# Attention block in float32: five pairs of output tiles projected by seven block products instead of eight, values of the tokens broadcast one by one

## The chip, the cores and the metric

The kernel runs on one core of one Trainium2 chip. The metric is the device time of one execution in microseconds, the median over several runs. The engines are TensorE (PE; its weight loads are listed as PEld), VectorE (DVE), ScalarE (ACT), GpSimd (POOL) and SyncE (SP, which here only issues DMAs).

## What is computed

Sixteen samples of 100 rows and 640 columns attend to a context of 722 rows and 384 columns, of which the last four are "tokens" with a path of their own. Everything is float32.

```python
query = hidden_states @ Wq
keyt = enc @ Wk                      # enc: the first 718 rows of the context
valt = enc @ Wv
hs = _mha(query, keyt, valt)         # 8 heads of 80
ca_q1 = jnp.einsum('btc,th->bch', ca, Wq_ca)     # ca: the last 4 rows
indices = np.linspace(0, CROSS_ATTENTION_DIM - 1, unet_size).astype(np.int64)
ca_q1 = ca_q1[:, indices, :]
ca_hs1 = _mha(ca_q1, residual, residual)
ca_q2 = ca_hs1 @ Wq
ca_k2 = ca @ Wk_ca
ca_v2 = ca @ Wv_ca
ca_hs2 = _mha(ca_q2, ca_k2, ca_v2)
out = (hs + ca_hs2) @ Wout + b_out + residual
```

The change concerns the last line, and how `ca_v2` reaches the engine that uses it.

## The kernel before

After a prologue that loads and prepares the weights, a loop runs over the 16 samples (`for b in range(B)`, L1122). Inside the loop the order of the instructions on every engine is the order in which they are written (a manual schedule, L1121); each engine works through its own list, and semaphores make it wait where data or a buffer is missing.

One sample on TensorE: scores (L620, three groups), the small products of the token path (L808, L746), the transposes of the sample before (L923), then the value and key blocks (L440, L471, interleaved; the next sample's keys are made here), the last chunk of keys (`last_keys`, L565), the output projection of a finished row tile if there is one (L951), the queries of the next two samples (L541, odd b only) and the attention products (L1317).

Output tiles. The 1600 output rows are cut into eleven tiles of 128 rows, one of 64 and one of 128 (`OC`, L33). A tile ends in sample `ENDS[r]`; `O_AFTER` (L37) says after which sample it is projected, so that no sample takes two of the full tiles. The samples of attention results are transposed (`transpose`, L916) into `hsT` tiles of five chunks of 128 columns by 128 rows. `load` of class `Last` (L897) brings the rows of x into `xn` and has GpSimd add the bias. `project` (L941) multiplies the five chunks with the two halves of Wout, ten matmuls of 128x128 by 128x320 into two banks of a PSUM pair; VectorE adds both halves to `xn` in one instruction (L970), and SyncE writes the rows out.

The order of things near the projection of a sample with 0 < b < 15 (L1237 to L1267) is `softmax3`, `values2`, value and key blocks, `subtract` and `exponential` of the three score tiles, `second.load`, `loads`, `load_m`, the third `subtract` and `exponential`, `last_keys`, `load_rest`, `second.softmax1`, `last.project`. Behind it GpSimd makes the masked keys (`keys`) and the sums of the context that the block products need (`enc_sums`).

Token path on GpSimd. `scores1` (L774) writes the first scores into `e1`; `Maximum` finds the row maximum and spreads it, where the last copy runs on VectorE, or on ScalarE if `scalar` is set. `load` of class `Second` (L824) broadcasts the values of the four tokens, 4x640 numbers, to 100 partitions: one DMA of 1000 KB from GpSimd's queue into `vb`, one sample ahead. `values2` (L861) does four products and three adds of 100x640 on GpSimd. `products` and `copy` (L740, L764) fill `y`, for which there are two buffers, as for `ca`.

PSUM has three pools of two buffers each: pairs of banks (`pair`), and single banks `psumk` and `psum1`; `psum` takes them in turn. The value and key blocks already use bilinear schemes with fewer products than blocks (`V_PLAN`, `K_PLAN`, L101 to L119).

Of the kernel before, what the change touches and what calls it, by code (L numbers as in the profile page):

```python
# [8 lines left out]
F32 = mybir.dt.float32  # L9
AF = mybir.ActivationFunctionType  # L10
ALU = mybir.AluOpType
# [4 lines left out]
NH, D = 8, 80  # L16
CAD, T = 384, 4
SK = 722 - T
P = 128
# [16 lines left out]
ENDS = [(lo + n - 1) // S for lo, n in OC]  # L36
O_AFTER = [b + 1 if b % 2 == 0 and b + 1 not in ENDS else b for b in ENDS]  # L37
HT = NH * T
# [94 lines left out]
def kernel(  # L133
# [66 lines left out]
    def hsT_tile(name):  # L200
        return main.tile([P, HC, P], F32, tag="hsT", name=name, bufs=2)

# [3 lines left out]
    def vb_tile(name):  # L206
        return main.tile([P, T, H], F32, tag="vb", name=name)

# [54 lines left out]
    wout_sb = const.tile([P, HC, H], F32, name="wout_sb")  # L263
    bias = const.tile([P, H], F32, name="bias")

    wvca_sb = enc_tile("wvca").rearrange("p f k -> p (f k)")[:, : CC * H].rearrange(
# [23 lines left out]
    load_first(0, CC, 2, slice(0, KT))  # L290
    tokens = vb_tile("tokens")
    cat_sb = tokens[:, CC, : CC * B * T].rearrange("p (c n) -> p c n", c=CC)
    wkca_sb = tokens[:, :CC, :]
    in_order(nc.sync.dma_start(out=cat_sb, in_=cat.rearrange("p c b t -> p c (b t)")))
# [6 lines left out]
    in_order(nc.sync.dma_start(out=xT, in_=xt[0:2].rearrange("b p c s -> p b c s")))  # L301
    ca_0 = small.tile([S, T, S], F32, tag="ca", name="ca_0", bufs=2)
    in_order(nc.sync.dma_start(out=ca_0, in_=cas[0].unsqueeze(0).to_broadcast([S, T, S])))
# [62 lines left out]

    ys = []
    for j in range(2):
        y = const.tile([S, NH, HT + 1], F32, name=f"y_{j}")
        nc.gpsimd.memset(y[:, :, HT:], 1.0)  # L370
        ys.append(y)

# [272 lines left out]
    def wait_for(ins, other):  # L645

        tc.add_manual_dep(
            ins.ins,
            other.ins.name,
            mybir.DependencyInfo(  # L650
                mybir.DependencyClass.Sync, mybir.DependencyReason.DATA
            ),
            reason="apart",
        )
# [70 lines left out]
    class Second:  # L725


        def __init__(self, b, xT, ca=None):
            self.b, self.xT = b, xT[:, b % 2]
            self.top = None  # L730

            self.ca = ca
            if ca is not None:
                return
            self.ca = small.tile([S, T, S], F32, tag="ca", name=f"ca_{b}", bufs=2)
            nc.sync.dma_start(
                out=self.ca, in_=cas[b].unsqueeze(0).to_broadcast([S, T, S])
            )
# [25 lines left out]
        def copy(self):  # L764
            b, y_ps = self.b, self.y_ps
            self.y = ys[b % 2]
            nc.scalar.copy(
                self.y[:, :, :HT].rearrange("p (u h) k -> p u h k", u=2),
                y_ps[:S, HT : 11 * HT].rearrange("p (u h k) -> p u h k", u=2, h=5)[
                    :, :, :4, :  # L770
                ],
            )
# [19 lines left out]
        def softmax1(self, n=8):  # L792

            if not self.top:
                self.top = Maximum(e1, f"1_{self.b}")
            self.top.go(n)
            if self.top.over is not None:
                nc.vector.tensor_tensor(e1[:S], e1[:S], self.top.over[:S], ALU.subtract)
# [24 lines left out]

        def load(self):  # L824
            b = self.b
            self.vb = vb = vb_tile(f"vb_{b}")
            nc.gpsimd.dma_start(
                out=vb[:S],
                in_=va_d[b * T : (b + 1) * T, :].unsqueeze(0).to_broadcast([S, T, H]),
            )  # L830

        def scores2(self):
# [28 lines left out]
        def values2(self, behind=None):  # L861

            b, p2, vb = self.b, self.p2, self.vb
            self.hs2 = hs2_tile(f"hs2_{b}")[:S]
            sums = self.hs2.rearrange("p (h d) -> p h d", h=NH)
            for t in range(T):
                to = sums if t == 0 else product_tile(f"hs2_{b}_{t}")[:S, :H].rearrange(
                    "p (h d) -> p h d", h=NH
                )
                first = nc.gpsimd.tensor_tensor(  # L870
                    to,
                    vb[:S, t, :].rearrange("p (h d) -> p h d", h=NH),
                    p2[:, :, t].unsqueeze(2).to_broadcast([S, NH, D]),
                    ALU.mult,
                )
                if t:
                    nc.gpsimd.tensor_tensor(sums, sums, to, ALU.add)  # L877
                elif behind:
                    wait_for(first, behind)

    def product_tile(name):
# [7 lines left out]
    class Last:  # L889
# [51 lines left out]
        def project(self, chunks=range(HC)):  # L941
            for r, xn in self.xn.items():
# [29 lines left out]
                )  # L972
                nc.sync.dma_start(out=o_v, in_=xn[:n])

        def project_few(self, r):
# [146 lines left out]
    for b in range(B):  # L1122
# [89 lines left out]
        elif b + 1 < B:  # L1212
# [4 lines left out]
            def both(n):  # L1217
                vv.go(n)
                kk.go(n)

            second.scores1(seen)
            if b == 1:
# [41 lines left out]
            if b + 2 < B:  # L1264
                enc_next = load_rest(b + 2, enc_next)
            second.softmax1()
            last.project()  # L1267
        else:
# [127 lines left out]
```

## Time and profile before

| what | value |
|---|---|
| runs | 943.98, 946.33, 944.89 us; median 944.89 |
| span of the profiled execution | 942.4 us |
| ScalarE busy | 364.7 us (39%) |
| mean granted clock of TensorE | 1.000 |
| TensorE in the first 60 us / 60 to 920 / the last 22.4 | 57.6 / 858.2 / 18.7 us busy |
| mean DMA rate, share of the span | 66 GB/s |
| attention products, L1317, from 204.82 (b = 2) | 6.67 us |
| GpSimd idle before `scores1`, L781, in all | 145.2 us, of which 125.0 until VectorE's maximum (L1156) |
| SyncE waiting to issue the next enc load, L228 | 598.8 us in 13 waits, for the value products |

The profile is of one execution, whose span runs from the first to the last instruction; the runs are timed from outside. A line of a timeline or of a group gives engine, line of the kernel, operation, what it writes and reads, the shapes and a count ("x20"); "idle before" is the time in which the engine had nothing to run, with the instruction that ended it. A float32 matmul leaves two records, each with its weight load.

### The profile page before, as it was taken

The page shows a single profiled execution, that of the slowest core. Times are in us where ns is not written, and L with a number is a line of the kernel's source. Part 1 is how long each engine was busy: PE and PEld are TensorE (multiplying, and loading weights), DVE is VectorE, ACT ScalarE, POOL GpSimd, SP SyncE. Part 2 cuts the span into 40 slices and gives each one's busy share as a digit, 9 for nine tenths or more (in the row PEclk, how much of TensorE's full clock was granted, in tenths as well). Part 3 has the DMA queues.
Part 4 walks back from the last instruction along what each step waited for, and adds up shares of the span by engine and source line. Part 5 has one row for each costly group of instructions (what it writes and reads, how often), then busy time and mean ns, then how long its engine had stood idle before and what let it go on. Part 6 is the DMA issues. An engine that isn't in the chain of part 4 may idle for free.

```text
span 942.4 us, 25629 instructions
## 1 busy us (share of the span) xinstructions
PE 934.5 (99%) x11215; PEld 796.2 (84%) x11215; DVE 674.0 (72%) x1084; ACT 364.7 (39%) x605; POOL 623.1 (66%) x565
## 2 busy tenths in 40 slices
PE   9999999999999999999999999999999999999998
PEld 6998979888797888989789887987989888897866
DVE  3559794977929688595955959578693886949684
ACT  1244443524334244433424334244431534334241
POOL 5857976776738757495873948657694576748514
PEclk9999999999999999999999999999999999999999
DMA  8822024040310404003050130403113030210300
GB/s 264 296 60 87 3 70 128 1 130 3 94 60 1 117 2 135 5 11 122 1 151 3 37 82 1 139 1 95 38 40 113 1 112 7 59 53 1 95 8 29
DMA packets 45367, 62.48 MB, mean 66 GB/s; under 512 B 13448, under 2 KB 37320, under 8 KB 43656
## 3 DMA queue, kind: packets, MB, share of 16 engines
q1 hardware_dynamic: 41720, 42.97, 15.2%
q0 software_dynamic: 2512, 16.72, 6.1%
q8 instruction: 88, 1.44, 0.6%
q10 hardware_dynamic: 1024, 1.15, 0.4%
q14 instruction: 23, 0.19, 0.1%
HBM read 55.26 MB, written 5.57 MB: 65 GB/s over the span
## 4 chain that ended last, share of the span: by engine, by line
PE 96%; DVE 3%; issue 0%; DMA 0%; ACT 0%; POOL 0%; ACTq 0%; DVEq 0%
PE s_ps L620 12%; PE a_ps L1317 12%; PE v_psA L440 10%; PE v_psB L440 8%; PE kT_ps L565 8%; PE k_psA L471 7%; PE q_ps L541 7%; PE o_ps L951 7%; PE k_psB L471 6%; PE v_psC L440 3%; PE k_psC L471 3%; PE y_ps L746 2%; PE v_ps L381 2%; PE v_psD L440 2%; PE v_psE L440 2%; PE k_psE L471 1%
## 5 line engine op out<-in xcount | busy, mean ns | idle before, releaser
L781 POOL TENSOR_TENSOR e<-ca,g 100x800 f32<-100x800 f32 x64 | 99.8, 1570 | 145.2 <-DVE most L1156 125.0
L870 POOL TENSOR_TENSOR hs<-vb,p 100x640 f32<-100x640 f32 x64 | 105.6, 1659 | 45.9 <-DVE p L856 32.5
L877 POOL TENSOR_TENSOR hs<-hs,hs 100x640 f32<-100x640 f32 x48 | 113.9, 2373 | 3.8
L1317 PEld LDWEIGHTS a_ps<-vs,st 120*36 120x36 f32 (+3 forms) x3072 | 109.1, 125 | 5.6 <-issue 5.5
L1317 PE MATMUL a_ps<-vs,st 120*36 120x81 f32 (+3 forms) x3072 | 111.9, 233 | 0.0
L440 PE MATMUL v_psA<-wv_sb,enc 128*120 128x320 f32 x352 | 109.5, 434 | 0.0
L506 POOL TENSOR_TENSOR enc<-enc 128x240 f32<-128x240 f32 x135 | 98.1, 736 | 16.9 <-DMA enc<-in_enct 9.8
L1144 DVE TENSOR_TENSOR st<-st,over 120x1600 f32<-120x1600 f32 x48 | 107.6, 2243 | 0.0
L637 ACT COPY st<-s_ps 120x800 f32<-120x800 f32 x64 | 49.7, 829 | 135.6 <-PE s_ps L620 135.6
L620 PE MATMUL s_ps<-qp,kT 32*120 32x100 f32 x3072 | 97.4, 263 | 0.0
L620 PEld LDWEIGHTS s_ps<-qp,kT 32*120 32x120 f32 x3072 | 94.7, 179 | 1.6 <-issue 0.2
L788 POOL TENSOR_TENSOR e<-e,e 100x800 f32<-100x800 f32 x48 | 90.4, 1884 | 3.8
L440 PE MATMUL v_psB<-wv_sb,enc 128*120 128x320 f32 x296 | 91.9, 433 | 0.0
L471 PE MATMUL k_psA<-enc,wk_sb 128*128 128x240 f32 x360 | 87.6, 366 | 0.0
L1329 DVE RECIPROCAL rs<-a_ps 100x4 f32<-100x4 f32 x32 | 5.8, 182 | 111.0 <-PE a_ps L1317 111.0
L1156 DVE TENSOR_TENSOR most<-most,st 120x800 f32<-120x800 f32 x64 | 66.2, 1034 | 24.1 <-ACT st L631 23.0
L1152 ACT ACTIVATE st<-st 120x1600 f32<-120x1600 f32 x48 | 73.9, 1539 | 22.3 <-DVE st L1144 22.2
L471 PEld LDWEIGHTS k_psA<-enc,wk_sb 128*128 128x128 f32 x360 | 68.2, 190 | 16.8 <-DVE kT L411 0.2
L440 PEld LDWEIGHTS v_psA<-wv_sb,enc 128*120 128x120 f32 x352 | 63.2, 183 | 22.6 <-issue 0.5
L471 PE MATMUL k_psB<-enc,wk_sb 128*128 128x240 f32 x300 | 73.1, 366 | 0.3 <-DVE sm L853 0.3
L440 PEld LDWEIGHTS v_psB<-wv_sb,enc 128*120 128x120 f32 x296 | 54.0, 183 | 21.9 <-DVE vs L411 0.4
L541 PE MATMUL q_ps<-xT,wq_sb 128*128 128x200 f32 x400 | 69.1, 333 | 0.0
(146 smaller groups left out, 1732.8 us busy)
## 6 DMA issues: line engine op xcount, KB each, us to landing
vb<-va_d POOLq DMA_DIRECT2D x16, 1000.0 KB, 7.4
enc<-in_enct SPq DMA_DIRECT2D x30, 240.0 KB, 3.9
enc<-in_enct SPq DMA_DIRECT2D x15, 360.0 KB, 3.6
xT<-in_xt SPq DMA_DIRECT2D x8, 500.0 KB, 4.3
rest<-in_enct SPq DMA_DIRECT2D x31, 120.0 KB, 6.6
xn<-in_x SPq DMA_DIRECT2D x11, 320.0 KB, 5.7
out<-xn SPq DMA_DIRECT2D x11, 320.0 KB, 3.2
ca<-in_cas SPq DMA_DIRECT2D x16, 156.2 KB
```

The source lines that it names most:

```text
L440: nc.tensor.matmul(at[0][j][:KN, : H // 2], a_form(self.enc, f)[:, j * KN : (j + 1) * KN], wv_there.get(f, wv_sb[:, W_AT[f]]), start=first ...
L471: nc.tensor.matmul(at[:, i * KT : (i + 1) * KT], wk_sb[:, W_AT[f], i], a_form(self.enc, f), start=(first and i == 0), stop=last, skip_grou ...
L506: nc.gpsimd.tensor_tensor(out, left, right, op)
L541: nc.tensor.matmul(q_ps[:, : 2 * S].rearrange("p (j s) -> p j s", j=2), wq_sb[:, c, n * P : (n + 1) * P], xT[:, :, c, :], start=(c == 0), ...
L565: nc.tensor.matmul(bank[:, i * KT : (i + 1) * KT], weights[c], a_raw(enc, u, c), start=(i == 0 and c == 0), stop=(c == CC - 1), skip_group ...
L620: nc.tensor.matmul(s_ps[r][:n, 256 * a + lo : 256 * a + hi], kT[rows, c, u, j * KN : (j + 1) * KN], rhs, start=(a == 0 and c == 0), stop=( ...
L781: first = nc.gpsimd.tensor_tensor(to, self.ca[:, t, :].unsqueeze(1).to_broadcast([S, NH, S]), g[:, :, t].unsqueeze(2).to_broadcast([S, NH, ...
L788: nc.gpsimd.tensor_tensor(e, e, to, ALU.add)
L870: first = nc.gpsimd.tensor_tensor(to, vb[:S, t, :].rearrange("p (h d) -> p h d", h=NH), p2[:, :, t].unsqueeze(2).to_broadcast([S, NH, D]), ...
L877: nc.gpsimd.tensor_tensor(sums, sums, to, ALU.add)
L1144: return nc.vector.tensor_tensor(st[i], st[i], top.over[:KN].unsqueeze(1).to_broadcast([KN, 2, ROWS]), ALU.subtract,)
L1317: nc.tensor.matmul(a_v[lo:hi, h % 4], st[i // 2][: KEYS[i], i % 2, h * S + lo : h * S + hi], block(i, h // 4)[: KEYS[i], h % 4], start=(i ...
```

## The change

Ten of the eleven full tiles are taken in five pairs (`PAIRS`): a pair is projected in the sample after the second tile's end, that is in samples 3, 6, 8, 11 and 13. The first four chunks of the two tiles are seen as a matrix of 2x2 blocks (tile by two chunks), Wout's first four chunks as 2x2 blocks (two chunks by half of the columns). The 2x2 product is made by seven block products with sums of blocks; the fifth chunk goes the usual way. The sums of the tiles' blocks and one sum of the weights are made on GpSimd in the sample of the pair, partly in place; weight sums are formed once in sample 2, and one is undone in the sample after each pair. After the last pair the overwritten quarter of Wout is loaded again. For SBUF space `y` and `ca` get one buffer, and `vb` two buffers of one token each: the first two tokens are loaded by GpSimd's queue, the others by SyncE's when a product has freed a buffer. `wkca` moves into a part of `wk_sb`. `hsT` gets three buffers. The remaining tiles (64 rows, the last full ones) are projected as before.

```diff
+PAIRS = {ENDS[r + 1]: r for r in range(0, 10, 2)}
+O_AFTER = [ENDS[r | 1] if r < 2 * len(PAIRS) else ENDS[r] for r in range(len(OC))]
...
-        return main.tile([P, HC, P], F32, tag="hsT", name=name, bufs=2)
+        return main.tile([P, HC, P], F32, tag="hsT", name=name, bufs=3)
...
-        return main.tile([P, T, H], F32, tag="vb", name=name)
+        return main.tile([P, H], F32, tag="vb", name=name, bufs=2)
...
+    wout2 = const.tile([P, 2, 2, H // 2], F32, name="wout2")
+    sum1 = const.tile([P, 2, P], F32, name="sum1")
...
-            self.ca = small.tile([S, T, S], F32, tag="ca", name=f"ca_{b}", bufs=2)
+            self.ca = small.tile([S, T, S], F32, tag="ca", name=f"ca_{b}")
...
-                self.top = Maximum(e1, f"1_{self.b}")
+                self.top = Maximum(e1, f"1_{self.b}", self.b - 2 in PAIRS)
...
         def load(self):
+            self.vb = [self.piece(nc.gpsimd, t) for t in range(2)]
+
+        def piece(self, engine, t):
             b = self.b
-            self.vb = vb = vb_tile(f"vb_{b}")
-            nc.gpsimd.dma_start(
-                out=vb[:S],
-                in_=va_d[b * T : (b + 1) * T, :].unsqueeze(0).to_broadcast([S, T, H]),
-            )
+            vb = vb_tile(f"vb_{b}_{t}")
+            engine.dma_start(
+                out=vb[:S], in_=va_d[b * T + t].unsqueeze(0).to_broadcast([S, H])
+            )
+            return vb
...
                 elif behind:
                     wait_for(first, behind)
+                if t + 2 < T:
+                    self.vb.append(self.piece(nc.sync, t + 2))
...
+        def sums(self):
+            r = PAIRS[self.b]
+            one, two = hsTs[r], hsTs[r + 1]
+            for out, left, right, op in (
+                (sum1, two[:, :2], two[:, 2:4], ALU.add),
+                (two[:, :2], sum1, one[:, :2], ALU.subtract),
+            ):
+                nc.gpsimd.tensor_tensor(out, left, right, op)
+
+        def project_pair(self):
...
+            both = pair(f"o_ps_{r}")
+            b1, b2 = psumk(f"o_ps1_{r}"), psumk(f"o_ps2_{r}")
+            b3, b4 = both[:, 0], both[:, 1]
...
+            def read(bank, j, k):
+                part = xn[r + j][:, k * (H // 2) : (k + 1) * (H // 2)]
+                nc.vector.tensor_tensor(part, bank[:, : H // 2], part, ALU.add)
+
+            product(b1, [(one[:, :2], w(0, 0))], True)
+            read(b1, 0, 0)
+            product(b2, [(one[:, 2:4], w(1, 0)), (one[:, 4:], last(0))], True)
+            read(b2, 0, 0)
+            nc.gpsimd.tensor_tensor(one[:, 2:4], one[:, 2:4], two[:, :2], less)
+            product(b1, [(two[:, :2], wout2[:, 0])], False)
+            read(b1, 1, 0)
+            nc.gpsimd.tensor_tensor(two[:, :2], two[:, 2:4], two[:, :2], less)
+            nc.gpsimd.tensor_tensor(wout2[:, 0], wout2[:, 0], w(0, 0), less)
+            product(b4, [(two[:, 2:4], wout2[:, 1]), (two[:, 4:], last(0))], True)
+            read(b4, 1, 0)
+            product(b1, [(sum1, w(0, 1))], False)
+            read(b1, 1, 1)
+            product(b3, [(two[:, :2], wout2[:, 0])], True)
+            read(b3, 1, 0)
+            product(b1, [(one[:, 2:4], w(1, 1)), (one[:, 4:], last(1))], False)
+            read(b1, 0, 1)
+            product(b3, [(two[:, 4:], last(1))], False)
+            read(b3, 1, 1)
...
+            if b == 2:
+                for o, left, right in (
+                    (forms[1], forms[1], forms[0]),
+                    (wout2[:, 0], forms[3], forms[1]),
+                    (wout2[:, 1], forms[2], wout2[:, 0]),
+                ):
+                    nc.gpsimd.tensor_tensor(o, left, right, ALU.subtract)
+            elif last.b - 1 in PAIRS:
+                nc.gpsimd.tensor_tensor(wout2[:, 0], wout2[:, 0], forms[0], ALU.add)
             second.scores1(seen)
...
+            if last.b in PAIRS:
+                last.sums()
+                second.softmax1(3)
+                last.project_pair()
+                if last.b == max(PAIRS):
+                    nc.sync.dma_start(
+                        out=forms[1],
+                        in_=wout[: 2 * P, H // 2 :].rearrange("(c p) n -> p c n", p=P),
+                    )
             second.softmax1()
-            last.project()
```

`w(i, k)` is the block of Wout with chunks 2i and 2i + 1 and half k of the columns, `last(k)` its fifth chunk, `one` and `two` are the `hsT` tiles of the pair, `product` issues one matmul for each chunk of its terms, and `forms` lists w(0, 0), w(0, 1), w(1, 0), w(1, 1).

## The prediction

> **What bounds the kernel now.** I read the totals first, then the chain of work that ended last, then the timeline around one output projection, then the DMA issues.
>
> ```profile
> PE 934.5 (99%) x11215; PEld 796.2 (84%) x11215; DVE 674.0 (72%) x1084; ACT 364.7 (39%) x605; POOL 623.1 (66%) x565
> ...
> PE 96%; DVE 3%; issue 0%; DMA 0%; ACT 0%; POOL 0%; ACTq 0%; DVEq 0%
> ```
>
> TensorE is busy for 934.5 of 942.4 us, and 96% of the chain is TensorE: a matmul taken out of the loop counts in full unless another engine then makes TensorE wait. One stretch of that chain, in sample 3 of the loop (b = 3, which will hold the first pair), in order of time (start, us, what):
>
> ```profile
> 249.45 3.65 PE kT_ps L565 x18
> 253.10 5.38 PE o_ps L951 x20
> 258.48 8.46 PE q_ps L541 x50
> ```
>
> Twenty records are ten matmuls (each float32 matmul leaves two). So a 128x128 by 128x320 matmul costs 0.538 us here; in the timeline below the projection starts at 252.93 and the queries follow at 258.32, 5.39 us later, which agrees. The mean granted clock is 1.000. The same stretch on the other engines:
>
> ```profile
> 235.24 1.54 POOL L908 TENSOR_TENSOR xn<-xn,bias 128x640 f32<-128x640 f32 x1
> ...
> 237.39 1.82 DVE L1144 TENSOR_TENSOR st<-st,over 120x1600 f32<-120x1600 f32 x1
> 237.55 4.02 POOL L870 TENSOR_TENSOR hs<-vb,p 100x640 f32<-100x640 f32 x2 [0.77 <-DVE p L856]
> ...
> 240.70 2.55 DVE L1144 TENSOR_TENSOR st<-st,over 120x1600 f32<-120x1600 f32 x1
> ...
> 241.64 3.02 POOL L877 TENSOR_TENSOR hs<-hs,hs 100x640 f32<-100x640 f32 x1
> ...
> 244.74 1.27 POOL L870 TENSOR_TENSOR hs<-vb,p 100x640 f32<-100x640 f32 x1
> ...
> 248.18 2.50 DVE L1144 TENSOR_TENSOR st<-st,over 120x1600 f32<-120x1600 f32 x1
> ...
> 249.07 3.02 POOL L877 TENSOR_TENSOR hs<-hs,hs 100x640 f32<-100x640 f32 x1
> ...
> 252.03 0.59 POOL L827 DMA_DIRECT2D vb<-va_d  x1
> ...
> 252.93 5.55 PE L951 MATMUL o_ps<-wout_sb,hsT 128*128 128x320 f32 x20
> ```
>
> Two things to see. GpSimd ends `values2` at 252.09, 0.84 us before the projection starts: no slack to speak of, and the new sums come behind it. And GpSimd and VectorE exclude each other: the second subtraction (240.70) takes 2.55 us for 1.82, ending 1.68 us after GpSimd's second product ends at 241.57; GpSimd's add (241.64) takes 3.02 us for 1.55. Of the four products in this stretch one takes 2.79 us and the rest 1.27:
>
> ```profile
> L870 POOL TENSOR_TENSOR hs<-vb,p x4: 1266/1273/2788, 237.5 to 247.7; 100x640 f32<-100x640 f32 x4
> ```
>
> So the first product was held by the first subtraction (ending at 239.21) and ended 1.13 us after it. The one that runs first finishes, the other waits.
>
> **The change part by part.**
>
> *Removed.* Counting `project_pair`: 2+3+2+3+2+2+3+1 = 18 matmuls of the old shape for 20. Five pairs: 10 x 0.539 = 5.39 us off TensorE.
>
> The page "Perfetto Trace Analysis", section "Identifying the Most-Contended Engine", speaks against this reading: matmul busy time is a poor measure, one should judge by the share of weight loads. Here that is 84%, and by it the 20 removed records would be worth 20 x 190 ns = 3.8 us, the mean weight load of this line, which would leave a sum 1.6 us worse. The chain's 5.38 us for 20 records decides for the larger value.
>
> *Moved on GpSimd, and what TensorE then waits for.* I follow sample 3. Two bias adds now stand before `values2`; the wait for p was 0.77 us, an add is 1.54, so the second runs from 236.86 to 238.40. The first subtraction (ready at 237.39) is held until then and ends 1.68 later, 240.08; the first product ends 1.13 after that, 241.21. The second subtraction is ready at about 241.0, once VectorE's two evacuations (1.03 us from 239.75 before) are done, takes its turn at 241.21 and ends at 242.89, before its old 243.25: VectorE has caught up. Second product 244.02; add 245.65 (0.08 gap, 1.55); third product 247.00; add 248.63; the third subtraction, ready at 248.18, runs to 250.31; fourth product 251.44; last add 253.07, 0.98 us later than before. Two DMA issues of 0.585 us instead of one: 254.18. The two sums are 128x256; between L506 (240 elements, 0.69) and L908 (640, 1.54) that is 0.72 each: ready at about 255.73.
>
> TensorE first has five matmuls that need no sum, 2.70 us, until 255.63; the weights of the sixth would load 0.20 earlier (252.73 against 252.93 at the first). They can load at 255.80 (0.07 for the signal, like the gap between two GpSimd instructions): 0.37 us lost. The sixth and seventh then run from 256.00 to 257.08, the last record ending 0.16 later (432 ns against a spacing of 270). Behind it GpSimd does 0.72 and 1.54 us with gaps: done at 259.65. TensorE has five matmuls (2.70) meanwhile and wants the weights of the next product at 259.57: another 0.15 us. So 0.52 per pair, 2.60 in all. The other GpSimd instruction in between (`one` minus `two`) ends before the seventh matmul does.
>
> Bounds: none of it if GpSimd's sums come 0.4 us sooner; 0.95 instead of 0.37 if the second subtraction loses its turn (second rival).
>
> *VectorE.* Eight reads of 320 for two of 640: 8 x 0.49 (L964 row) against 2 x 0.82, behind the matmuls. Each is finished before its bank is written again, since three other matmuls (1.6 us) lie between. One exception: at b = 13 the first query chunk takes the bank of `b1`, whose last read ends about 0.16+0.07+0.49 us after its product while one matmul (0.54) remains: 0.2 us once. The rest of `softmax1` (two instructions of 1.0 us) goes behind the reads; its exponential is wanted only in the next sample's `softmax2`, behind attention and scores, 14 us on. The broadcast copy of 0.98 us moves to ScalarE (39% busy).
>
> *The tokens' values.* Per sample SyncE issues two broadcasts of 250 KB as a buffer comes free. Behind them in SyncE's queue stand the next xT, ca and enc loads; enc waits until 248.67 anyway and the other two are not used before the next sample. The third token's load starts when the first product ends, 240.34 now, and is wanted at 244.74: 4.4 us of cover (4.5 in a pair's sample, 241.21 to 245.73). The price is bounded by these rows:
>
> ```profile
> vb<-va_d POOLq DMA_DIRECT2D x16, 1000.0 KB, 7.4
> rest<-in_enct SPq DMA_DIRECT2D x31, 120.0 KB, 6.6
> out<-xn SPq DMA_DIRECT2D x11, 320.0 KB, 3.2
> ```
>
> Nearest is `out`: one transfer of that size alone on the same queue, 3.2 us, and this one will be alone too; `rest` runs beside 1000 KB of `vb`. I take 3.2: hidden by 1.2 us. The far end, 6.6, is the slower rival.
>
> "DMA: Bandwidth & Descriptors", section "Bandwidth", speaks against cutting a transfer up: batch to 1 MiB or more. Its fit (2.0 us plus bytes over 436 GB/s, stated for GpSimd's path) gives an estimate of 2.6 us for 250 KB, four times that per sample for 4.3 us in one piece; the sum would still not change, as 2.6 fits the cover.
>
> *At nothing.* Forming the weights at b = 2 (three of 1.54 us) and undoing them (one) stand before `scores1`, where GpSimd idles 11.2 us at b = 2 and 8 to 18 us in the samples after a pair. Without that cover they would hold `scores1` (ending at 235), wanted only by `softmax1` at 250.6. One `ca` buffer: the load waits for `scores1` of the sample before, done at 235 where the load is issued near 250. One `y`: the copy follows matmuls that TensorE has behind it. The reload of a quarter of the weights after the last pair has two samples. Samples 2, 4, 10, 12 and 14 lose their projection and go straight to attention: the third exponential (L1152, 250.77 for 1.54 us) ends 0.6 us before that point (252.31 against 252.93), and GpSimd's idle time ahead of `scores1` shrinks from 7.6 to 2.2 us, so both just hold.
>
> *Sum.* 942.4 - 5.39 + 2.60 + 0.2 = 939.8 for the profiled span. The median of the runs, 944.89, lies 2.5 above that span; on it: 942.3.
>
> **The rivals.**
>
> *TensorE hardly waits:* GpSimd's chain is up to 0.4 us quicker than I make it. For it: the held instructions are known only from ends that overlap by 0.1 us. Then 944.89 - 5.39 = 939.5, with little stalls up to 940.8.
>
> *The turn goes the other way:* at 241.21 the second product starts ahead of the waiting subtraction. I have 0.2 us between them. VectorE's later evacuations come 1.0 us late; that of k_psC ended at 244.55 and its next matmul came at 244.68, so TensorE loses 0.95 us there, and the sums are then in time: 1.1 per pair, 5.5 in all, 945.2: no change. Against it: the add at 241.64 waited for the subtraction that had been waiting longer.
>
> *Slower: the third token is late.* Place: GpSimd's third product in a pair's samples. Every microsecond by which the load takes longer than 4.5 passes to the sums and to TensorE. From 5.0 us (2.6/5 more) the gain is gone; from 5.6 the kernel is slower by over 0.3%; at 6.6 it is 5 x 2.1 = 10.4 us, 952.7. For it: all loads of the sample on one queue, one DRAM row read for 100 partitions. Against: that queue is empty between 237 and 248 (no issue by SyncE), and 1000 KB take only 7.4.
>
> **How the numbers follow.** 0.3% is 2.8 us, about what a measurement of this kernel can tell from no change: the lines lie at 942.06 and 947.7. My case (0.2 to 0.8 us lost per pair, 941 to 944) gets 0.55, hardly any wait 0.20, the turn lost 0.13, the slower rival 0.12. My case straddles the upper line, 0.25 of it below. Faster: 0.20 + 0.25 = 0.45; same 0.30 + 0.13 = 0.43; slower 0.12. The range leaves out most of the slower rival and the tip of the first: 940.0 to 945.5.
>
> **What would show it.** Paired matmuls of this shape: 90 (180 records) in five blocks of 9.7 us plus waits, in place of ten of 5.4. In the waits of `o_ps`: GpSimd's sum (`sum1`, `hsT`) as the releaser with about 0.4 us at the sixth matmul, and 0.1 to 0.2 with the weights. The first subtraction 0.9 longer, the last `values2` add about 1 us later against the block. If the product of `vb` waits for a DMA, the slower rival is on; if k_psC waits for VectorE near 1 us, the second. If TensorE idles anywhere else in the loop, something I have costed at nothing is wrong.

## The result, and the profile after

| | before | after |
|---|---|---|
| median of 14 runs each | 944.42 us | 942.67 us |
| lowest and highest | 943.95, 946.33 | 941.78, 944.7 |
| span of the profiled execution | 942.4 us | 940.1 us |

The ratio is 0.9978, with an interval of 0.9971 to 0.9986: 2.1 us by the ratio, small, but the interval lies wholly below 1. The forecast of 942.3 us and its range held. By the line of 0.3% that the prediction drew this is "same" (0.43), not "faster" (0.45). The way there was not the one I had worked out, as the rest shows.

The totals and the shares of the chain in the page of the changed kernel:

```profile
PE 931.7 (99%) x11195; PEld 792.4 (84%) x11195; DVE 687.0 (73%) x1099; ACT 372.9 (40%) x615; POOL 669.3 (71%) x613
...
PE 87%; POOL 6%; DVE 4%; issue 1%; ACT 1%; DMA 0%; DVEq 0%; POOLq 0%
```

Twenty records fewer on TensorE, and its busy time fell by 2.8 us. GpSimd has 46 us more work (71% for 66%) and appears in the chain, 6% for nothing before. So TensorE now waits for GpSimd somewhere. The timeline of the first pair (b = 3), TensorE's matmuls and then GpSimd's sums:

```profile
248.14 2.86 PE L1010 MATMUL o_ps<-wout_sb,hsT 128*128 128x320 f32 x10
251.27 2.42 PE L1010 MATMUL o_ps<-wout,hsT 128*128 128x320 f32 x8 [0.27 <-POOL hsT L991]
253.53 0.70 PE L1010 MATMUL o_ps<-wout_sb,hsT 128*128 128x320 f32 x2
...
249.67 0.74 POOL L991 TENSOR_TENSOR sum<-hsT 128x256 f32<-128x256 f32 x1
250.49 0.72 POOL L991 TENSOR_TENSOR hsT<-sum,hsT 128x256 f32<-128x256 f32 x1
```

Five matmuls (ten records) start at 248.14 and would be through at 250.83, after 5 x 0.538 us. The sixth wants a sum that ends at 251.21, and starts at 251.27. The nine matmuls from 253.53 on, with the weights' difference among their operands, end at 258.37 where the queries begin: 4.84 us, 9 x 0.538, no time lost. The whole block takes 10.23 us for 18 x 0.538 = 9.68. The same two waits in the list of waits of the weight loads (sum in us, how many, the longest):

```profile
PEld o_ps L1010 <- POOL hsT L991: 2.9, 5, 0.8
...
PEld o_ps L1010 <- POOL wout L1031: 1.2, 5, 0.2
```

To see where the rest went I used a property of this kernel: between fixed points of a sample, TensorE's stretches repeat to about 0.02 us. In the kernel before, attention takes 6.91 us from its first record to the first score, the scores 7.28, the token scores 0.68, and the value and key blocks 25.10 from their first `k_psA` to `kT_ps`, in every sample from b = 1 on (one single 0.76 for 0.68 apart). "Behind b" below means what follows the attention of sample b. Whatever a stretch takes more is a wait. Counted in this way against the kernel before less 5.38 us:

| stretch of TensorE, changed kernel | longer by, us |
|---|---|
| pairs in b = 3, 6, 8, 11, 13 | 0.56, 0.26, 0.21, 0.25, 0.38: 1.66 |
| blocks behind b = 2 | 0.82 |
| scores and token scores behind b = 10 | 0.65 |
| token scores behind b = 12 | 0.27 |
| start, up to the attention of b = 1 | -0.23 |

(The blocks behind b = 2 take 26.02 us for 25.10; 0.09 of the difference was lost just ahead of them in the kernel before.) The gain of 5.38 us less 1.66, less 1.74, plus 0.23 is 2.2 us, for the 2.3 between the spans. The 1.74 us behind b = 2, 10 and 12, samples that lost their projection, are a cost that I had put at nothing. The experiments are mostly about it.

One execution of each kernel was profiled, and the runs of one kernel spread by up to 2.9 us (the changed kernel's from 941.78 to 944.70). So the size of a single loss is that of one execution. What carries the argument is what moves with an edit, or repeats over many traces.

### The profile page after: what moved, and what is told of

Same layout as the page of the kernel before. It is cut to its first block, busy times and chain, and to the rows that moved or that the text cites. A ratio compares the mean times of both kernels' runs of the same rounds, so it can differ in the third digit from the quotient of the medians.

```text
span 940.1 us, 25799 instructions
## 1 busy us (share of the span) xinstructions
PE 931.7 (99%) x11195; PEld 792.4 (84%) x11195; DVE 687.0 (73%) x1099; ACT 372.9 (40%) x615; POOL 669.3 (71%) x613
## 4 chain that ended last, share of the span: by engine, by line
PE 87%; POOL 6%; DVE 4%; issue 1%; ACT 1%; DMA 0%; DVEq 0%; POOLq 0%
PE a_ps L1409 12%; PE s_ps L623 12%; PE v_psA L443 9%; PE v_psB L443 7%; PE q_ps L544 7%; PE kT_ps L568 7%; PE k_psA L474 6%; PE k_psB L474 5%; PE o_ps L1010 5%; PE v_psC L443 3%; PE k_psC L474 2%; POOL hs L876 2%; PE v_ps L384 2%; PE y_ps L749 2%; DVE most L1229 1%; PE v_psD L443 1%
## 5 line engine op out<-in xcount | busy, mean ns | idle before, releaser
L876 POOL TENSOR_TENSOR hs<-vb,p 100x640 f32<-100x640 f32 x64 | 119.6, 1877 | 52.5 <-DVE p L862 41.2
L509 POOL TENSOR_TENSOR enc<-enc 128x240 f32<-128x240 f32 x135 | 106.9, 801 | 21.5 <-DMA enc<-in_enct 14.4
L1217 DVE TENSOR_TENSOR st<-st,over 120x1600 f32<-120x1600 f32 x48 | 103.3, 2154 | 0.0
L883 POOL TENSOR_TENSOR hs<-hs,hs 100x640 f32<-100x640 f32 x48 | 100.5, 2095 | 3.8
L1229 DVE TENSOR_TENSOR most<-most,st 120x800 f32<-120x800 f32 x64 | 68.5, 1070 | 23.6 <-ACT st L634 22.5
L544 PEld LDWEIGHTS q_ps<-xT,wq_sb 128*128 128x128 f32 x400 | 67.9, 190 | 1.1 <-issue 0.5
```

What stands on the lines that cost most here:

```text
L509: nc.gpsimd.tensor_tensor(out, left, right, op)
L544: nc.tensor.matmul(q_ps[:, : 2 * S].rearrange("p (j s) -> p j s", j=2), wq_sb[:, c, n * P : (n + 1) * P], xT[:, :, c, :], start=(c == 0), ...
L876: first = nc.gpsimd.tensor_tensor(to, self.vb[t][:S].rearrange("p (h d) -> p h d", h=NH), p2[:, :, t].unsqueeze(2).to_broadcast([S, NH, D] ...
L1217: return nc.vector.tensor_tensor(st[i], st[i], top.over[:KN].unsqueeze(1).to_broadcast([KN, 2, ROWS]), ALU.subtract,)
L1229: most_now = nc.vector.tensor_tensor(most[:KN], most[:KN], st[i][:, u], ALU.max)
```

## The experiments

All ratios are to runs of the kernel before on the same chip. "Span" is that of the profiled execution.

**The order of the tiles (e1).** The changed kernel, but the pairs' samples project both tiles with ten plain products each, and no sums and no weights are formed. The tokens' loads and the single buffers of `y` and `ca` stay:

```diff
-            if last.b in PAIRS:
-                last.sums()
-                second.softmax1(3)
-                last.project_pair()
...
             second.softmax1()
+            last.project()
```

> The changed kernel with its order of tiles (two tiles projected together in samples 3, 6, 8, 11, 13, none in 2, 4, 10, 12) but every tile projected by eight block products in the old way, no sums, no weights formed. Theory: taking the projection out of samples 2, 4, 10, 12 costs time by itself, because GpSimd's sums of the context then meet VectorE's maximum in the next sample: 0.8, 0, 0.65 and 0.3 us lost in samples 3, 5, 11 and 13, so 1.5 to 1.8 us slower than the kernel before (about 946.0 for 944.4), with a wait of k_psE for VectorE of about 1.3 us in sample 3. Rival (the placement is free and the 1.7 us were lost to the new GpSimd work or the token loads): 944.4 within 0.4.

Measured: 945.79 us, ratio 1.0019 [1.0010, 1.0027], span 944.5 for 942.4. With as many matmuls as before, the kernel is slower by 1.8 us. So putting projections together in some samples, and leaving none in others, costs without any of the sums, and as much as the 1.74 us above (e2 rules out the tokens' loads; the single buffers were not tried alone). The total is as expected, the place and with it the reason are not: only 0.07 us behind b = 2, but 1.68 us in scores and token scores behind b = 10, and 0.31 behind b = 12.

**The tokens' values alone (e2).** The kernel before with the change's two buffers and its `load`, `piece` and `values2`:

```diff
-        return main.tile([P, T, H], F32, tag="vb", name=name)
+        return main.tile([P, H], F32, tag="vb", name=name, bufs=2)
...
+                if t + 2 < T:
+                    self.vb.append(self.piece(nc.sync, t + 2))
```

> The kernel before with only the values of the tokens broadcast one by one in two buffers. Theory: hidden, 944.4 within 0.4, with the third token's product never waiting in samples 2 to 15. Rival (the token loads hold GpSimd and through it VectorE): 0.5 to 1.7 us slower.

Measured: 944.32 us, ratio 1.0004 [0.9995, 1.0013], span 942.3. The loads are hidden, and the cut into four costs nothing that can be seen.

**The sums ahead of the token loads (e3).** One move in the changed kernel:

```diff
+            if last.b in PAIRS:
+                last.sums()
             second.load()
...
             if last.b in PAIRS:
-                last.sums()
                 second.softmax1(3)
```

> The changed kernel with the two sums of a pair put ahead of GpSimd's two DMA issues (1.1 us) instead of behind them. Theory: the wait of the sixth matmul for the sums (0.5 to 0.8 us of weight-load idle time in each pair) goes, and only the wait for the weights' difference (0.1 to 0.2 us) stays: 0.7 to 1.2 us faster than the changed kernel, about 941.7. Rival (the next instruction behind, the difference of weights, is late by as much, so the wait moves): 942.7 within 0.3.

Measured: 940.18 us, ratio 0.9962 [0.9949, 0.9974], span 938.6. The first pair in its timeline, TensorE and then GpSimd:

```profile
247.72 2.85 PE L1010 MATMUL o_ps<-wout_sb,hsT 128*128 128x320 f32 x10
250.41 2.32 PE L1010 MATMUL o_ps<-wout,hsT 128*128 128x320 f32 x8
...
248.96 0.72 POOL L991 TENSOR_TENSOR hsT<-sum,hsT 128x256 f32<-128x256 f32 x1
```

The second sum ends at 249.68, 0.73 us before the sixth matmul, which now follows at 250.41, 2.69 us after the first: 5 x 0.538. The queries begin at 257.40, so the block takes 9.68 us. All five pairs lose nothing any more, the last one (b = 13) included: 1.66 us came back, more than the 0.7 to 1.2 us expected. The two DMA issues of 1.10 us had stood in front of the sums, and nothing waits for them. Yet the span fell by 1.5 only, as other stretches changed: behind b = 10 the excess is now 1.37 us for 0.65, behind b = 2 it is 0.35 for 0.82.

**Two buffers for the rest of the context (e4).** My theory then was that GpSimd's sums of the context (`enc_sums`, L509), late for want of the projection's 5.4 us, meet VectorE's maximum of the next scores in the samples behind a lost projection. An earlier load of what they wait for should help:

```diff
-        return main.tile([P, len(A_REST), KT], F32, tag="rest", name=name)
+        return main.tile([P, len(A_REST), KT], F32, tag="rest", name=name, bufs=2)
...
                 m_next = load_m(b + 2)
+                enc_next = load_rest(b + 2, enc_next)
             subtract(2)
```

(For space, `mb` gets one buffer and the tile of the idle matmuls lies in another.)

> The changed kernel with two buffers for the rest of the context, loaded ahead of the last chunk of keys instead of behind it (the room comes from one buffer for mb instead of two and from a shared tile for the idle matmuls). Theory: the context sums end 2 to 5 us earlier in samples 2, 4, 10 and 12, VectorE's maximum in the next sample runs in its usual 2.0 us for two, and the 1.7 us lost in samples 3, 11 and 13 come back: about 941.0. Rival (the loss is not from this meeting): 942.7 within 0.3.

Measured: 942.96 us, ratio 0.9983 [0.9974, 0.9992], span 939.7; the excess is still 0.38 us behind b = 2 and 0.55 behind b = 10, and nothing behind b = 12. In the profile half of the loss came back, in the median nothing. At b = 2 the sums waited for `mb` first, as the timelines of the changed kernel show; GpSimd, then VectorE, then TensorE:

```profile
203.19 2.00 POOL L721 TENSOR_TENSOR m<-mb,hmask 128x64 f32<-128x64 f32 x5 [4.20 <-DMA mb<-m_d]
...
213.27 4.37 POOL L509 TENSOR_TENSOR enc<-enc 128x240 f32<-128x240 f32 x3
...
212.57 2.87 DVE L1229 TENSOR_TENSOR most<-most,st 120x800 f32<-120x800 f32 x2 [1.36 <-ACT st L634]
...
216.10 2.38 DVE L1229 TENSOR_TENSOR most<-most,st 120x800 f32<-120x800 f32 x2
...
228.08 1.08 PE L474 MATMUL k_psE<-enc,wk_sb 128*128 128x240 f32 x4 [0.28 <-DVE vs L414]
```

Masked keys 4.2 us late, the last sums end at 217.64. Two pairs of VectorE's maximum beside them take 2.87 and 2.38 us, where the kernel before has, GpSimd and then VectorE,

```profile
202.75 2.15 POOL L718 TENSOR_TENSOR m<-mb,hmask 128x64 f32<-128x64 f32 x5 [4.05 <-DMA mb<-m_d]
...
213.41 2.13 POOL L506 TENSOR_TENSOR enc<-enc 128x240 f32<-128x240 f32 x3
...
218.19 2.02 DVE L1156 TENSOR_TENSOR most<-most,st 120x800 f32<-120x800 f32 x2 [1.48 <-ACT st L631]
```

VectorE's later evacuations (its additions of finished PSUM banks to `vs` and `kT`) come late by that, and `k_psE` waits for one. In the kernel before `mb` is as late, but GpSimd's sums ended 2.7 us ahead of this maximum.

The thirteen traces together bear the meeting out. Four such maxima take 3.96 us undisturbed. In the 119 stretches between b = 2 and b = 13 where they take at most 0.1 us more, the blocks lose nothing. Where they take 1.23, 0.89, 0.75 and 0.44 us more (changed kernel b = 2, e11 b = 12, e3 b = 2, e7 b = 2) and TensorE has not stopped before them, the blocks lose 0.92, 0.60, 0.44 and 0.14: all but 0.3 us (at b = 4 up to 0.46 us more cost at most 0.03). How long `mb` takes at b = 2 is not the edits' doing: GpSimd waits 4.20 us for it in the changed kernel and 2.15 to 2.46 in e1, e3 and e4, which all issue it in the same place. So the 0.82 us is at the high end, and what e3 and e4 gained behind b = 2 is not shown to be theirs.

**Where TensorE stops behind b = 10 and 12.** There the profile names no engine. Pieces of the scores' and token scores' timelines behind b = 10, in e1:

```profile
659.88 0.68 PE L623 MATMUL s_ps<-qp,kT 32*120 32x100 f32 x16
661.34 0.57 PE L623 MATMUL s_ps<-qp,kT 32*120 32x100 f32 x13 [0.78 <-issue]
...
669.13 0.46 PE L811 MATMUL z_ps<-y_sb,e 100*4 100x33 f32 x33 [0.17 <-issue]
```

and in e3:

```profile
656.62 1.08 PE L623 MATMUL s_ps<-qp,kT 32*120 32x100 f32 x27
657.86 0.35 PE L623 MATMUL s_ps<-qp,kT 32*120 32x100 f32 x3 [0.17 <-issue]
...
665.64 0.38 PE L811 MATMUL z_ps<-y_sb,e 100*32 100x33 f32 x22 [0.52 <-issue]
```

"Issue" is time for which the profile has no releaser. The gaps come in the middle of a group of like matmuls, in e1 behind 16 of them and in e3 behind 27. I numbered all records of TensorE (weight loads, matmuls and 210 semaphore instructions) in order of time. Every such gap, in e1, in e3 and in the changed kernel, stands at a number that leaves 193 or 194 when divided by 256 (15,810; 16,066; 16,321; 19,138). And in all of them the last packet of one DMA queue had ended 1.3 to 1.5 us earlier. That queue's line, in the changed kernel (packets, MB, share of the DMA engines):

```profile
q8 instruction: 88, 1.44, 0.6%
```

88 packets of 16 KB for 22,600 records: one for each 256. TensorE was waiting for its own instructions. Below, an edge is the record at which the instructions of a new packet begin. The packet that is wanted at one edge starts only at about the time when TensorE passes the edge before it. In the undisturbed stretches of the kernel before it starts within 1.2 us of that edge, takes about 1 us (0.9 to 1.5) and ends 1.4 us or more ahead of the edge at which it is wanted; behind b = 10 it started 2.46 us after the edge in the changed kernel, and 3.16 in e1. TensorE goes through 256 records in 2.8 to 4.6 us in these stretches, so these packets came too late.

The Trainium skill, "Runtime: NRT & Kernel Launch", section "Instruction fetch mechanics", says that an engine's instructions are refilled in blocks of 16 KiB, 256 instructions, and that the crossing of a block's edge is mostly hidden. The block agrees with the 88 packets. That it is mostly hidden agrees with the kernel before, whose loop loses at two edges only (0.08 and 0.09 us). Behind b = 10 and 12 of the changed order it does not hold: up to 0.9 us at an edge, one to three edges in a sample.

**Moving the edges (e5 and e6).** If late packets are the cause, useless instructions ahead of everything must move the gaps. The five idle matmuls at the start become

```diff
-    for _ in range(5):
+    for _ in range(3):
         nc.tensor.matmul(idle_ps[:, :P], idle, idle, start=True, stop=True)
+    for _ in range(40):
+        nc.tensor.matmul(
+            idle_ps[:32, :33], idle[:100, :32], idle[:100, :33], start=True, stop=True
+        )
```

on top of e3, and four and seven of the two kinds in e6.

> The kernel of e3_sums_first, with three large idle matmuls and 40 of 32x33 ahead of the first products instead of five large ones: 38 more matmuls, four records each, so 152 more TensorE instructions in front of everything. Theory (TensorE waits for its own instructions): in the samples b = 10 and b = 12 the records stop at the numbers 15,810, 16,066, 16,321 and 19,138 of all TensorE records, which leave 193 or 194 when divided by 256, in four kernels alike, and each time 1.3 to 1.5 us after the end of a 16 KB packet of the instruction queue. 152 more in front move these places by 152 records. From the crossing times and the packets of e3: scores and token scores of b = 10 fall from 7.92 and 1.41 us to 7.28 and 0.68, at b = 12 0.76 goes to 0.68, another 0.0 to 0.4 us may appear near 205 us (b = 2); span 938.6 - 1.4 + 0.2 = 937.4, 0.3 us for the idle matmuls either way. Rival (these gaps come from the data: late exponentials, sums or semaphores): the gaps stay at b = 10 and b = 12 and the span stays within 0.3 of 938.6.

> The same with four large idle matmuls and seven small ones: 24 more TensorE instructions in front. Theory of the instruction supply: a bad place. The edges then fall where the packets were seen to start latest; by the crossing times of e3, gaps of 0.4 to 3.1 us in all, most of it near 203.5 us (b = 2, the scores), smaller ones near 207, 550, 657 and 774 us; all gaps at record numbers that leave 193 or 194 when divided by 256; span 938 to 941. Rival (the gaps come from the data): nothing changes but the start, span within 0.3 of 938.6 with the gaps of b = 10 where they were.

Measured for e5: 940.77 us, ratio 0.9967 [0.9955, 0.9980], span 940.0. Behind b = 10 the gaps are gone; scores 7.28 us, token scores 0.68:

```profile
658.36 1.10 PE L623 MATMUL s_ps<-qp,kT 32*120 32x100 f32 x32
...
665.64 0.75 PE L811 MATMUL z_ps<-y_sb,e 100*32 100x33 f32 x64
```

Behind b = 12 the token scores are back at 0.68 too, and in their place attention has 0.33 us more there and 0.19 at b = 2, at records 18,625 and 4,801, which leave 193. The span rose all the same, for two reasons. The pad cost 2.0 us at the start, not 0.2 (below). And where TensorE no longer stops, the blocks behind b = 10 and b = 12 take 0.45 and 0.34 us more: now VectorE's maximum meets GpSimd's late sums there, 2.77 us for 2.01. A gap ahead of them had hidden that.

Measured for e6: 941.51 us, ratio 0.9972 [0.9963, 0.9981], span 937.2. In the profiled execution the gap behind b = 10 stands behind 15 score matmuls instead of 27:

```profile
655.56 0.67 PE L623 MATMUL s_ps<-qp,kT 32*120 32x100 f32 x15
656.78 0.68 PE L623 MATMUL s_ps<-qp,kT 32*120 32x100 f32 x17 [0.55 <-issue]
```

24 records more in front, 12 matmuls earlier: it kept its number, 15,810, and not its place in the work. With e5 that settles the cause of these gaps. What I expected near 203.5 us (1.5 us and more) is not in this execution, which is the fastest of eleven; their median lies 2.6 us above it, and what the others waited for was not recorded.

**The masks' load first (e7), and both (e8).** On top of e3, and of e3 with e5's pad:

```diff
+            if b + 2 < B:
+                m_next = load_m(b + 2)
             second_next, enc_next = loads()
-            if b + 2 < B:
-                m_next = load_m(b + 2)
```

> The kernel of e3_sums_first, with the load of the next mask columns (mb) ahead of the loads of the context in SyncE's order. Theory (in the sample after b = 2 VectorE's maximum is held by GpSimd's sums of the context, which are late because the masked keys wait for mb): GpSimd's wait for mb after the second b = 2 transfer (2.46 us in e3, 4.20 in the changed kernel) goes to under 0.3, the sums end at 212.5 or earlier and no longer meet the maximum; the blocks of the next sample fall from 25.54 to 25.10 us, so span 938.6 - 0.45 = 938.15. Rival (the sums wait for the rest of the context anyway, as in e4, and meet the maximum all the same): blocks 25.4 to 26.0, span 938.5 to 939.1.

> The edits of e5_pad152 and e7_masks_first together on e3_sums_first. If both theories hold and the two losses do not meet: 938.6 - 1.2 - 0.45 = 937.0 for the span, about 938.9 for the median, faster than the kernel before by 0.6%. If only the instruction supply is right 937.4; if neither, 938.6.

Measured for e7: 940.23 us, ratio 0.9961 [0.9948, 0.9973], span 938.6. GpSimd no longer waits for `mb` at b = 2, but then for the context itself:

```profile
199.76 1.40 POOL L721 TENSOR_TENSOR m<-mb,hmask 128x64 f32<-128x64 f32 x5
201.81 0.69 POOL L509 TENSOR_TENSOR enc<-enc 128x240 f32<-128x240 f32 x1 [0.65 <-DMA enc<-in_enct]
204.30 0.71 POOL L509 TENSOR_TENSOR enc<-enc,rest 128x240 f32<-128x240 f32 x1 [1.79 <-DMA rest<-in_enct]
```

The sums end at 213.93 (expected 212.5, 217.64 in the changed kernel), and the blocks behind b = 2 take 25.25 us for 26.02 in the changed kernel and 25.54 in e3. The wait for the masks goes with the edit; the meeting does not wholly, as the first two maxima still take 2.46 us for 2.0. How much of the 0.3 us is the edit's stays open, for e5 and e6, with the masks' load in its old place, have 25.17 and 25.18 there. The span did not fall, because edges behind b = 9, 10 and 12 took 0.35, 0.32 and 0.52 us.

Measured for e8: 940.38 us, ratio 0.9962 [0.9949, 0.9974], span 938.6, not 937.0: the pad's 1.5 us at the start again. In the loop nearly all is gone: 0.05, 0.12, 0.09 and 0.13 us over the undisturbed stretches.

**A cheaper pad (e9), and the weights on VectorE (e10).** In e9 the small matmuls write three groups of rows in turn:

```diff
-    for _ in range(40):
+    for i in range(40):
+        lo = 32 * (i % 3)
         nc.tensor.matmul(
-            idle_ps[:32, :33], idle[:100, :32], idle[:100, :33], start=True, stop=True
+            idle_ps[lo : lo + 32, :33],
...
```

and e10 has, on top of it,

```diff
-            nc.gpsimd.tensor_tensor(wout2[:, 0], wout2[:, 0], w(0, 0), less)
+            nc.vector.tensor_tensor(wout2[:, 0], wout2[:, 0], w(0, 0), less)
```

> The kernel of e8_both; only the 40 small idle matmuls write three groups of 32 output rows in turn instead of one. In e5 the 80 records took 4.61 us (58 ns each, into one group) and held the first value products until 7.25 us, where 0.2 us had been expected; the token scores of e3, which change groups, take 0.68 us for 64 records (10.6 ns). Theory (the records of one group follow each other, those of several overlap): 0.9 us for the 80, the first products start near 3.6 us again, and the span of e8, 938.6, falls by 1.5 to 1.9: 936.9. Rival (the small records cost 58 ns at the start of a kernel whatever they write): 938.6 again. The gaps of the instruction supply stay where they are in e8, since the count of instructions is the same.

> The kernel of e9, and the difference of the weights in a pair (1.54 us on GpSimd, behind two sums) on VectorE. Theory (five times 0.24 us of idle weight loads, my second wait of a pair): VectorE needs about 0.82 us for these 640 elements, as in L970 before, and is done ahead of the eleventh product, so the wait goes and the span is 0.7 to 1.2 us below that of e9: 936.0. Rival (VectorE's reads of the banks come later by 0.8 us and TensorE waits for a bank instead): same as e9 or up to 1 us above it.

Measured for e9: 939.74 us, ratio 0.9953 [0.9940, 0.9965], span 938.0: with e10 the fastest of all, 4.4 us (0.5%) below the kernel before. The pads in the timelines of e5 and of e9:

```profile
2.71 4.61 PE L1076 MATMUL idle_ps<-idle 100*32 100x33 f32 x80
```

```profile
2.71 1.75 PE L1077 MATMUL idle_ps<-idle 100*32 100x33 f32 x80
```

58 ns a record became 22, between the theory's 10.6 and the rival's 58; the first keys start 1.4 us earlier than in e8. Of that 0.25 us is gone by the first attention, with a gap of 0.59 us at record 1,474, and 0.79 went into two edges in attention, 0.40 at b = 2 and 0.39 at b = 12.

Measured for e10: 939.80 us, ratio 0.9955 [0.9941, 0.9968], span 937.7. The difference takes 1.04 us on VectorE and the wait of the weight loads for it is gone from the list, all five times 0.24 us. The pairs take as long as in e9, 9.69 us where queries follow and 9.78 where attention does, all five of them. The theory was wrong: that idle of the weight loads had lain under the matmul still running, and was never TensorE's loss.

**Transfers that nobody reads (e11).** What makes the packets late? e9, with four useless transfers at b = 4 and b = 10:

```diff
+            if b in (4, 10):
+                for i in range(4):
+                    nc.sync.dma_start(
+                        out=noise[b // 10, i],
+                        in_=x.rearrange("b s n -> (b s) n")[i * P : (i + 1) * P],
+                    )
```

> The kernel of e9_rotated, with four transfers of 320 KB from one place of DRAM to another that nothing reads, issued by SyncE behind the rest of the context in b = 4 (from about 315.6 us on) and b = 10 (from about 651). In e9 the stretches behind them run without a gap: attention, scores and token scores 6.91, 7.28 and 0.68 us. No engine waits for these transfers, and no instruction is added on TensorE. Theory (the packets of TensorE's own instructions queue behind data on the DMA engines): the packets that are due near 317.3, 321.9, 655.2 and 659.2 us start later than the 0.5 to 1.1 us after their edge seen in e9, and the three stretches grow by 0.3 to 3 us at b = 4 and as much at b = 10, in gaps at record numbers that leave 193 or 194 when divided by 256; the median rises by 0.6 to 6 us over 939.7. Rival (the gaps have to do with the place in the program alone, or with data that arrive late): the stretches stay at 6.91, 7.28 and 0.68 and the median within 0.5 of 939.7, but for the start of GpSimd's sums if the rest of the context lands later.

Measured: 940.75 us, ratio 0.9963 [0.9949, 0.9977], span 939.0; 1.0 us above e9. SyncE's issues in the timeline, and the gap behind b = 4 that e9 does not have:

```profile
315.44 2.48 SPq L1364 DMA_DIRECT2D noise<-in_x  x4
...
321.87 0.72 PEld L624 LDWEIGHTS s_ps<-qp,kT 32*120 32x120 f32 x24 [0.19 <-issue]
```

The scores take 0.27 us more behind b = 4, just under the lower end I gave, and 0.66 behind b = 10; the gaps are at records 7,618 and 16,066, both leaving 194. The packet wanted there started 2.43 us after its edge, 1.12 in e9. (Elsewhere the two executions differ by up to 0.5 us in a stretch, up and down, which cancels; every run of e11 lies above every run of e9.) No engine waits for these transfers, so it is the traffic alone: data transfers delay TensorE's instructions. Whether they meet in the DMA engines or in the memory behind them is not shown.

The traces also point at loads that no edit moved. In the changed kernel SyncE issues the rows of x for both tiles of a pair right behind the rest of the context in b = 2, 10 and 12; the kernel before loads at most one tile's rows there, and only behind its projection's output. Behind b = 10, the changed kernel and then the kernel before:

```profile
652.09 0.90 SPq L915 DMA_DIRECT2D xn<-in_x  x2
```

```profile
659.58 0.43 SPq L907 DMA_DIRECT2D xn<-in_x  x1
```

The data of the two tiles end at 656.98 us in the changed kernel, 659.00 in e1 and 655.56 in e3; the packet that TensorE then lacks starts at 656.86, 659.00 and 655.56. b = 4 lost its projection too and has the same loads of the context, but no rows of x: there no packet starts more than 1.4 us after its edge in any trace but e11's (1.4 in e5, 1.2 in e8 and e9, whose edges fall among the loads), and nothing is lost. So the lost projection alone does not cost a stop; the rows of x, which the change also moved, look like the rest of the reason. No run moved them elsewhere.

## Why the prediction held, point by point

*The ten matmuls removed: right.* A block of 18 takes 9.68 us where nothing disturbs it (e3), 0.538 us each; the weight loads' 3.8 us would have been wrong.

*The tokens' values at nothing: right.* e2 shows no cost. A transfer from GpSimd's queue took 4.1 us in the median. For SyncE's, by which the third token comes, the page has no landing; its data were through 2.3 to 2.7 us after the issue began, not 3.2, and the third product followed at 4.5 us in the pairs' samples without a wait: the cover was as long as I had put it. The slower rival is out.

*The turns of GpSimd and VectorE: right.* The second subtraction did run before the second product in all five pairs' samples (236.36 to 238.45 us in b = 3, the product ending at 239.59), and no evacuation was late there, so the second rival is out too.

*"0.37 lost" at the sixth matmul: the right wait, of about the right size.* It was 0.21 to 0.56, in the mean 0.33 us, and e3 takes all of it away.

*"Another 0.15 us" for the weights' difference: wrong.* The weight loads did wait, 0.24 us each time, but TensorE's matmuls did not (4.84 us for nine), and e10 without that wait gains nothing. I took the moment at which the weights are wanted for the moment at which time is lost. With the 0.2 us at b = 13, which e3 does not show either, the pairs came to 1.66 us for my 2.8.

*"Samples 2, 4, 10, 12 and 14 lose their projection [...] so both just hold": the step that failed.* It cost 1.74 us in the profiled execution. I had looked at two covers, and both held: the third exponential, and GpSimd's idle time ahead of `scores1`, of which 1.1 to 4.8 us were left. Two others were under the projection's 5.4 us. GpSimd's last sums of the context ended 2.7 us ahead of VectorE's maximum at b = 2, and now overlap it (the lines under e4): 0.82 us. And the projection's twenty slow records lay between the sample's burst of loads and the fast records of attention and scores; without them, and with the rows of x for two tiles in the burst, TensorE meets its instruction edges while the loads still run (e1, e5, e6, e11): 0.92 us. I said that an idle TensorE elsewhere in the loop would show something costed at nothing to be wrong; it did.

*The sum.* 939.8 was forecast for the span and 940.1 measured, since 1.74 us too little stood against 1.14 too much for the pairs and 0.23 gained at the start. The step from span to median was off too: a run lies 1.7 us above its span here (941.78 for 940.1), while my 2.5 came from a median of three runs that 14 runs put 0.5 lower; and the profiled execution was the fastest of the changed kernel's 14. These also cancelled. That the total held was in good part luck: the terms on either side of it were off by over 1 us each.

Open: why `mb` needs 6.9 us from its issue to its use at b = 2 and 3.7 at b = 4, and between 3.5 and 6.9 at b = 2 in the kernels that issue it in the same place; which of a sample's loads a packet waits behind, as only added traffic was tried; and what the median execution of the changed kernel, 0.9 us above the profiled one, waited for.

## What to carry to other kernels

A long operation on the bounding engine is also cover for everything that runs beside it: before it is moved, list for that place which engines end in its shade, by how much each, and what transfers run in it. Where TensorE issues hundreds of small matmuls in a row (here 256 records in under 4.6 us), its own instructions are a stream that can run dry; gaps with no releaser at record numbers that repeat by 256 show it, and large loads are better placed beside slow instructions than beside fast ones. An idle weight load is a loss only if the matmul in front of it has ended.

## What was not expected of the hardware

- TensorE stops at an edge, every 256 records, when the 16 KB packet with its next instructions is late: up to 0.9 us each time, 1.7 us in all behind b = 10 in e1. In these traces the packet starts at about the time when TensorE passes the edge before, so one block is in reserve.
- Where these edges fall decides in which samples TensorE stops (e5, e6, e9). What that is worth in time drowns in the spread of the runs: eleven of e6, with 24 useless instructions in front, lie between 938.94 and 943.57 us; five of e5, with 152, between 940.10 and 941.96; five of e8, with 152 and the masks first, between 940.23 and 940.56.
- Small matmuls at the start (100x32 by 100x33) took 58 ns a record into one group of rows and 22 into three in turn; the token scores, which change groups, take 10.6 in the loop.
